# One hybrid block on one core: routing weights in four copies in DRAM, v rows straight from the plain normalised rows

## The chip, the core and the metric

The kernel runs on one core of a Trainium2 chip. A core has a matrix engine (TensorE, in the profile PE, with its weight loads as PEld), a vector engine (VectorE, DVE), a scalar engine with table functions (ScalarE, ACT), a general engine (GpSimd, POOL) and a queue that issues transfers (SyncE, SP). Each works through its own instructions in order; between engines they wait on semaphores. The metric is the device time of one execution in microseconds, lower is better. Before the change the median of three runs is 1353.25 us (1351.0 to 1355.0).

## What is computed

Eight sequences (B = 8) of 512 rows of 128 numbers pass through four residual layers: a selective scan ("mamba"), a mixture of eight experts, a windowed attention with 16 heads of 8, and the mixture of experts again, with the same weights.

```python
x = x + mamba(_layernorm(x))
x = x + ffn(_layernorm(x))
x = x + attention(_layernorm(x))
x = x + ffn(_layernorm(x))

# ffn: every expert sees every row
router_probs = softmax(x @ w_router)
gate_weights = softmax(x @ w_gating / 0.1)
g = einsum('bsh,ehf->ebsf', x, w_gate)          # 8 experts, 128 -> 512
u = einsum('bsh,ehf->ebsf', x, w_up)
h = silu(g) * u
expert_out = einsum('ebsf,efh->ebsh', h, w_down)   # 512 -> 128
cw = router_probs * gate_weights
cw = cw / (sum(cw) + 1e-9)
out = einsum('ebsh,bse->bsh', expert_out, cw)

# attention: q, k, v = x W + b; windowed softmax; out @ Wo + bo
```

Everything is fp32, and every expert is computed for every row, so the expert products are most of the arithmetic.

## The kernel before

**Precision.** A product of two fp32 matrices is made from three products in a faster format: `matmul3` (lines 489 to 494) splits both sides into a high and a low part (fp32r) and adds high x high, low x high and high x low. Small products use plain fp32.

**Layers and buffers.** Activations lie transposed in SBUF (128 features x 512 rows of a sequence). Between layers a sequence's rows are written to DRAM and read again.

**The expert stream** (`ffn_stream`, 1123 to 1325) is the backbone: for both passes k, eight sequences b, eight experts e and four chunks f of 128 hidden units, it makes g and u (three 128x512 products each), then, two to four chunks later (SHALLOW and DEPTH), the chunk's part of y. In `hidden` (1246) ACT takes the silu, DVE multiplies by u, ACT or DVE casts the high part, POOL or DVE makes the low part. The first sequence runs its first four experts in two halves of 256 rows, so that it can start earlier.

**Routing weights.** `ffn_prep` (1023 to 1100) normalises the rows, transposes them (`tp_f`), makes the logits (`lps`, `rps`), the softmaxes, and the combined weights cw, which are laid out for each tile of 128 rows with the eight experts beside each other. They are transposed (`cps`), copied to SBUF (`cwt`) and written to a DRAM tile `cwd` of 4 tiles x 8 experts x 128. For each expert, `spreads` (1197 to 1214) later reads its 512 weights back from DRAM into all 128 partitions (`cwb`), in pieces of 128 weights; the read is issued when the stream reaches the expert's last chunk and a buffer is free. `weighted` (1138) multiplies y by it on DVE and adds it to `acc` on POOL (for the first expert it writes acc directly, and y's PSUM bank is free then).

**Attention.** `attention_prep` (1341 to 1398) normalises a sequence's rows, transposes them (`tp_a`) and splits them into high and low parts. Then come q (`aqk..._0`) and k (`aqk..._1`): `matmul3`, a bias, a split into three bf16 pieces, written to DRAM in twelve transfers (`put`). Then v: `matmul3` into `avp`, bias on ACT into `avf`, four transposes into `avt`, a copy on ACT into `avs`, and one transfer `avd` to DRAM. The buffers of tag "rest" (`arest`, `avf`, `avs`) are one and the same. `attention` (1420 to 1708) reads q, k and v back for windows of about 100 queries, makes scores twice (`as` for the maxima, `aw` for the weights), and the weighted values (`ao`); `joined` (1613) makes the output product `aout`.

**Who sets the order.** The order of every engine's instructions is written out at build time by a planner in the kernel's own source: `Clock` (133 to 250) holds an estimate of when each engine is done, from costs of its own; `Lanes` (285 to 373) holds generators ("lanes"), each of which yields the engine that it needs next. `tick` runs whichever lane can start soonest. A lane that needs TensorE waits, beside its inputs, a while for other small products that it may stand next to (`joins`, by default JOIN; JOIN_MAX for the rows of maxima, JOIN_ATT for `attention_prep`), unless it is due. `HELD`, `SECOND`, `PRESS` and `FIRST` say by how much one kind of lane may go ahead of another; `SECOND` is that of the second half of the first sequence. Where TensorE would stand idle, filler products are put: `warm` ones before the stream starts, and `idle` ones after a planned gap of WARM_GAP, up to the stream position WARM_TO (1.0 is one sequence). `Clock.run` also estimates when a transfer lands. These estimates decide only the order; on the chip, semaphores do.

Two helpers that the steps name: `normalised` (542 to 563) makes the transposed rows in two parts, and with `plain=True` also a plain fp32 copy of them in the normalised rows' buffer; that buffer exists once (LNB = 1) and is passed on with `lanes.give("ln", ...)`. `load_x` and `store_x` (448, 457) move a sequence's rows.

Of the kernel before, what the change touches and what calls it, by code (L numbers as in the profile page):

```python
# [8 lines left out]
F32 = mybir.dt.float32  # L9
# [3 lines left out]
AF = mybir.ActivationFunctionType  # L13
ALU = mybir.AluOpType
# [4 lines left out]
P = 128  # L19
# [68 lines left out]

TABLES = {AF.Silu: (18,), AF.Exp: (0, 6), AF.Ln: (6,), AF.Tanh: (0, 18)}
INF = float("inf")  # L90
LAGS = {"T": 0.2, "A": 0.15, "V": 0.15, "P": 0.08}
TO_PE = 0.11
SAME = 0.125
# [2 lines left out]
FIRST = 0.6  # L96
LATE = 0.3
SIDE = 0.5
JOIN = 2.0
JOIN_DUE = 0.0  # L100
JOIN_MAX = 6.0
JOIN_ATT = 3.0
JOIN_END = 2.0
MOST = 6
OTHERS = 4
AT_FIRST = 7
WARM = 3.5
WARM_GAP = 0.25
WARM_TO = 1.5
SECOND = 0.2  # L110
PRESS = 0.4
HELD = 0.18
MAMBA_DUE = 0.9
PREP_DUE = 0.9
ATT_LEAD = 2.5
# [13 lines left out]
class Clock:  # L129
# [105 lines left out]
    def run(self, key, name, out, args, kw, after, wait):  # L235
        c = self.cost(key, name, out, args, kw)
        start = max(self.end[key] + wait, after, self.now if key == "T" else self.based(key))
        if key == "T":
            if start > self.end["T"] + 2.4:
                self.cold = start  # L240
            if start < self.cold + 3.4:
                c *= 2
        if key in "VP" and self.shares(key, name, out, args):
            start = self.with_port(start, c)
        self.end[key] = start + c
        if key == "S":
            start = max(start, self.now)
            row = out.shape[-1]
            rows = out.shape[0] * size(out) // row
            each = max(row * (2 if out.dtype == BF16 else 4), 512)  # L250
            move = rows * each / 200e3
            self.moved = max(self.moved, start + c + 0.8) + move
            return self.moved + 0.6 + move
        self.hop[key] = start + c
        return start + c + LAGS[key]

# [121 lines left out]
def block_kernel(ctx: ExitStack, tc: tile.TileContext, x, pack_a, pack_b, pack_c, w_qkv, mask, mask_t, w_o,  # L378
# [52 lines left out]
    def side(shape, name):  # L431
        return (yield from sides((shape, name)))[0]
# [590 lines left out]
    def ffn_prep(k, b, xc, t0=0, nt=NT):  # L1023

        nm = f"f{k}_{b}_{t0}"
        cols = slice(t0 * P, (t0 + nt) * P)

        def halves():
            if t0 == 0:
                ready[k, b] = [fp.tile([P, L], F32R, tag=f"xt{i}", name=f"xt{i}_{nm}") for i in range(2)], 0  # L1030
            return [t[:, cols] for t in ready[k, b][0]]

        if (k, b, t0) == (0, 0, 0):
            done["quiet"] = 0.0
        *_, xf = yield from normalised(xc, nm, halves, nt, t0 + nt == NT, quick=nt < NT, plain=True)
        if (k, b, t0) == (0, 0, 0):
            done.pop("quiet", None)
            done["calm"] = 0.0
        if t0 == 0:
            done["cw", k, b] = dram.tile([NT, NE, P], F32, tag="cwd", name=f"cwd_{nm}", bufs=3), 0.0, 0  # L1040
        cwd = done["cw", k, b][0]
        ready[k, b] = ready[k, b][0], cols.stop
        wr, = routes

        lps = yield from side([P, P], f"lps_{nm}")
        for t in range(nt):
            e = pe.matmul(lps[32 * t : 32 * t + 32], wr, xf[:, t * P : (t + 1) * P], start=True, stop=True)
        lanes.give("ln", e)
        yield "V"
        n = 32 * nt  # L1050
        lt = fp.tile([P, P], F32, tag="lt", name=f"lt_{nm}", bufs=1)
        freed(dve.tensor_copy(lt[:n], lps[:n]))
        yield "T"
        rps = yield from side([P, NT, 32], f"rps_{nm}")
        pe.transpose(rps.rearrange("p t c -> p (t c)")[:, :n], lt[:n], ident[:n, :n])
        yield "V"
        pr = fp.tile([P, 2 * NT, NE], F32, tag="pr", name=f"pr_{nm}")
        s8 = fp.tile([P, 2 * NT], F32, tag="s8", name=f"s8_{nm}")
        pr, s8 = pr[:, : 2 * nt], s8[:, : 2 * nt]
        prv = pr.rearrange("p (t s) e -> p t s e", s=2)  # L1060
        s8v = s8.rearrange("p (t s) -> p t s", s=2)
        logits = rps[:, :nt, : 2 * NE].rearrange("p t (s e) -> p t s e", s=2)
        dve.tensor_reduce(s8v, logits, AX.X, ALU.max)
        yield "V"
        freed(dve.tensor_tensor(prv, logits, s8v[:, :, :, None].to_broadcast([P, nt, 2, NE]), ALU.subtract))

        yield lambda: clock.table in TABLES[AF.Exp] or pos[0] >= k * B + b - LATE
        yield "A"
        act.activation(pr, pr, AF.Exp)
        if (k, b) == (0, 0) and t0:  # L1070
            clock.hold = clock.now


        yield "V"
        cw = fp.tile([P, NT, NE], F32, tag="cw", name=f"cw_{nm}")[:, :nt]
        s4 = fp.tile([P, NT], F32, tag="s4", name=f"s4_{nm}")[:, :nt]
        z = fp.tile([P, NT], F32, tag="z", name=f"z_{nm}")[:, :nt]
        dve.tensor_reduce(s8, pr, AX.X, ALU.add)
        pool.tensor_tensor(cw, prv[:, :, 0], prv[:, :, 1], ALU.mult)
        yield "V"  # L1080
        dve.tensor_reduce(s4, cw, AX.X, ALU.add)
        pool.tensor_tensor(z, s8v[:, :, 0], s8v[:, :, 1], ALU.mult)
        pool.tensor_scalar(z, z, 1e-9, 1.0, ALU.mult, ALU.mult)
        yield "P"
        pool.tensor_tensor(s4, z, s4, ALU.add)
        yield "V"
        dve.reciprocal(s4, s4)
        yield "P"
        pool.tensor_tensor(cw, cw, s4[:, :, None].to_broadcast([P, nt, NE]), ALU.mult)
        yield "T"  # L1090
        cps = yield from side([NT * NE, P], f"cps_{nm}")
        n = nt * NE
        pe.transpose(cps[:n], cw.rearrange("p t e -> p (t e)"), ident)
        yield "V"
        cwt = fp.tile([NT * NE, P], F32, tag="cwt", name=f"cwt_{nm}")
        freed(dve.tensor_copy(cwt[:n], cps[:n]))
        yield "S"
        e = sp.dma_start(out=cwd[t0 : t0 + nt].rearrange("t e p -> (t e) p"), in_=cwt[:n])
        done["cw", k, b] = cwd, e, cols.stop

    pos = [0.0]
# [21 lines left out]
    def ffn_stream():  # L1123
# [73 lines left out]
        def spreads():  # L1197

            for k in range(2):
                for b in range(B):  # L1200
                    todo = passes(k, b)
                    for i, (e, cs) in enumerate(todo):
# [6 lines left out]
                        n = cs.stop - cs.start  # L1209
                        cwb = fp.tile([P, L], F32, tag="cwb", name=f"cwb{k}_{b}_{e}_{cs.start}", bufs=2)[:, :n]  # L1210
                        state["cwb", (k, b, e, cs.start)] = cwb, sp.dma_start(
                            out=cwb.rearrange("p (t q) -> p t q", q=P),
                            in_=cwd[None, cs.start // P : cs.stop // P, e, :].to_broadcast([P, n // P, P]),
                        )

        def chunks(cs):
# [111 lines left out]
    def attention_consts():  # L1328
        raw = qp.tile([P, 3, P], F32, tag="rest", name="wqkv")
        there = sp.dma_start(out=raw, in_=w_qkv) + 1.5  # L1330
        yield "A", there
        consts = []
        for i, nm in enumerate(("wq", "wk", "wv")):
            consts.append((yield from split_const(raw[:, i, :], P, nm)))
            yield "A"
        return consts

    scaling = HD ** -0.5
# [2 lines left out]
    def attention_prep(b, consts):  # L1341
# [2 lines left out]
        def halves():  # L1344
            return [qp.tile([P, L], F32R, tag=f"t{i}", name=f"axt{b}_{i}") for i in range(2)]

        xt = yield from normalised(xc, f"a{b}", halves)
        stacks = []
        for m, (bcol, order) in enumerate(((B_BQ, Q_PIECES), (B_BK, K_PIECES))):
            pp = yield from side([P, L], f"aqk{b}_{m}")  # L1350
# [7 lines left out]
            def put(piece, pi):  # L1358
                js = [j for j, o in enumerate(order) if o == pi]
                places = slice(js[0], js[-1] + 1, js[1] - js[0] if len(js) > 1 else 1)  # L1360
                for s in range(2):
                    half = piece[64 * s : 64 * s + 64, None, :]
                    sp.dma_start(
                        out=qd[s, places].rearrange("j r t -> r j t"),
                        in_=half.to_broadcast([64, len(js), L]),
                    )

            ps_ = [qp.tile([P, L], BF16, tag="pc", name=f"apc{b}_{m}_{i}", bufs=3) for i in range(3)]
            rest = qp.tile([P, L], F32, tag="rest", name=f"arest{b}_{m}")
# [7 lines left out]
            dve.tensor_tensor(ps_[2], rest, ps_[1], ALU.subtract)  # L1377
            put(ps_[1], 1)
            yield "S"
            put(ps_[2], 2)  # L1380
            stacks.append(qd.rearrange("s j (d p) t -> s (j d) p t", p=NPAIR))
            yield "T"
        vp = yield from side([P, L], f"avp{b}")
        matmul3(vp, consts[2], xt)
        yield "A"
        vf = qp.tile([P, L], F32, tag="rest", name=f"avf{b}")
        freed(act.activation(vf, vp, AF.Identity, bias=pb[:, B_BV : B_BV + 1]))
        yield "T"
        vt = yield from side([P, NT, P], f"avt{b}")
        for t in range(NT):  # L1390
            pe.transpose(vt[:, t, :], vf[:, t * P : (t + 1) * P], ident)
        yield "A"
        vs = qp.tile([P, NT, P], F32, tag="rest", name=f"avs{b}")
        freed(act.copy(vs, vt))
        yield "S"
        vd = dram.tile([L, P], F32, tag="vd", name=f"avd{b}", bufs=2)
        e = sp.dma_start(out=vd.rearrange("(t p) d -> p t d", p=P), in_=vs)
        heads[b] = stacks[0], stacks[1], vd, e + 3.0

    def attention_preps():  # L1400
# [460 lines left out]
```

## Time and profile before

| | |
|---|---|
| runs | 1351.0, 1353.25, 1355.0 us (median 1353.25) |
| profiled execution | 1351.62 us, its span 1349.8 us, mean granted clock 0.996 |
| first expert product (g) | starts at 34.31 us of the span |
| expert products u, g, y | 451.5, 448.3, 445.5 us busy |
| h on POOL | 640.0 us busy in 492 additions of 1310 ns |
| table loads on ACT | 109 and 16 under another line |
| transfers | 107.75 MB, 80 GB/s over the span; the 124 reads of cwb 256 KB each |
| packets under 2 KB | 226616 of 230861 |

How to read it: the profile is one execution, taken by the hardware profiler. "Busy" is the time in which an engine worked on an instruction; matmuls are pipelined, so the durations of successive ones overlap, and their start-to-start distance says what one costs. Nearly all instructions carry line 269, since a helper there issues them; groups are told apart by the names of their tiles, output first ("avt<-ident,avf": into avt, from the identity and avf). A number in brackets behind "idle before" is how long the engine stood idle ahead of a group, with who released it. The granted clock is the share of TensorE's clock that the chip let through.

### The profile page before, as it was taken

The numbers are of one execution on the slowest core, as the hardware profiler recorded it, in microseconds if no ns is written. First come the engines' busy times: TensorE is split into PE (matmuls) and PEld (weight loads), VectorE is DVE, ScalarE is ACT, GpSimd is POOL, SyncE is SP. The second block draws the span as 40 slices with busy tenths as digits, with TensorE's granted clock in tenths as the row PEclk, the third lists the DMA queues.
The fourth block names the chain that finished last, engine by engine and source line by source line (L and its number), as shares of the span: only waits on it lengthen the run. The fifth ranks groups of instructions, "written<-read, shape, count | busy, mean of one in ns | idle before, by whom it ended". The sixth has DMA issues, their size and how long they took to land.

```text
span 1349.8 us, 29533 instructions
## 1 busy us (share of the span) xinstructions
PE 1328.9 (98%) x10261; PEld 1053.3 (78%) x10261; DVE 1036.8 (77%) x3114; ACT 964.7 (71%) x1694; POOL 940.4 (70%) x1042
## 2 busy tenths in 40 slices
PE   7999999999999999999999999999999999999998
PEld 7877778788788877777777777777777777778887
DVE  6887888688888867898788887888888787855443
ACT  7768576867787556777777777777877767765654
POOL 5877576776767757666766767767677676777776
PEclk9999999999999999999999999999999999999999
DMA  3321304232112242344345444454544434222111
GB/s 126 95 72 38 87 24 101 62 81 73 45 48 56 63 85 54 73 97 118 79 103 111 99 106 100 104 109 89 118 91 104 119 71 88 61 69 55 40 40 40
DMA packets 230861, 107.75 MB, mean 80 GB/s; under 512 B 86417, under 2 KB 226616, under 8 KB 230712
## 3 DMA queue, kind: packets, MB, share of 16 engines
q1 hardware_dynamic: 230712, 105.87, 33.9%
q8 instruction: 81, 1.33, 0.4%
q14 instruction: 68, 0.56, 0.1%
HBM read 77.64 MB, written 27.79 MB: 78 GB/s over the span
## 4 chain that ended last, share of the span: by engine, by line
PE 89%; POOL 3%; ACT 3%; issue 3%; DVE 2%; DMA 0%; POOLq 0%; DVEq 0%
PE u L269 25%; PE y L269 25%; PE g L269 25%; PE ao L269 2%; PE aw L269 2%; PE as L269 2%; POOL h L269 1%; PE mo L269 1%; PE aqk L269 1%; ACT h L269 1%; DVE h L269 1%; PE mde L269 1%; PE aout L269 1%; PE yp L269 1%; ACT L269 1%
## 5 line engine op out<-in xcount | busy, mean ns | idle before, releaser
L269 POOL TENSOR_TENSOR h<-h,h 128x512 fp32r<-128x512 f32 x492 | 640.0, 1310 | 279.0 <-ACT h L269 219.4
L269 PE MATMUL u<-xt_f,wu 128*128 128x512 f32 (+1 forms) x1584 | 451.5, 395 | 3.5 <-ACT h L269 2.7
L269 PE MATMUL g<-xt_f,wg 128*128 128x512 f32 (+1 forms) x1584 | 448.3, 393 | 2.1 <-ACT h L269 1.9
L269 PE MATMUL y<-h,wd 128*128 128x512 f32 (+1 forms) x1584 | 445.5, 392 | 1.4 <-POOL h L269 0.8
L269 DVE TENSOR_TENSOR h<-u,h 128x512 f32<-128x512 f32 x420 | 285.9, 686 | 157.5 <-PE u L269 109.3
L269 ACT ACTIVATE h<-g 128x512 f32<-128x512 f32 x512 | 303.4, 597 | 123.2 <-PE g L269 100.1
L269 ACT CAST h<-h 128x512 fp32r<-128x512 f32 x437 | 268.4, 619 | 171.2 <-DVE h L269 169.6
L269 PEld LDWEIGHTS g<-xt_f,wg 128*128 128x128 f32 x1584 | 288.5, 189 | 70.3 <-ACT h L269 3.0
L269 PEld LDWEIGHTS y<-h,wd 128*128 128x128 f32 x1584 | 288.3, 188 | 70.2 <-POOL h L269 1.4
L269 PEld LDWEIGHTS u<-xt_f,wu 128*128 128x128 f32 x1584 | 286.6, 189 | 71.7 <-ACT h L269 4.1
L269 POOL TENSOR_TENSOR acc<-acc,cwb 128x512 f32<-128x512 f32 (+1 forms) x114 | 148.0, 1298 | 52.5 <-DVE cwb L269 33.8
L269 ACT ACT_TABLE_LOAD x109 | 139.8, 1283 | 24.7 <-PE g L269 23.2
L269 DVE CUSTOM_DVE_ANT_0 amasked<-as,maskq 128x60 f32<-128x60 f32 x640 | 95.4, 213 | 5.0 <-PE as L269 4.8
L269 DVE TENSOR_TENSOR cwb<-y,cwb 128x512 f32<-128x512 f32 (+1 forms) x116 | 77.5, 668 | 16.0 <-PE y L269 14.4
L269 DVE TENSOR_TENSOR apt<-aw,maskk 125x400 f32<-125x400 f32 (+2 forms) x160 | 88.1, 570 | 0.0
L269 DVE SCALAR_TENSOR_TENSOR h<-h,g 128x512 f32<-128x512 f32 x92 | 62.3, 681 | 27.0 <-ACT h L269 26.6
L269 ACT ACTIVATE apt<-apt 125x400 f32<-125x400 f32 (+2 forms) x160 | 81.5, 540 | 0.4
L269 DVE SCALAR_TENSOR_TENSOR h<-u,h 128x512 f32<-128x512 f32 x92 | 62.6, 683 | 3.3 <-PE g L269 0.5
L269 DVE DVE_READ_ACCUMULATOR2_ANT amx<- 128x1 f32 x640 | 52.1, 81 | 0.0
L269 DVE CAST h<-h 128x512 fp32r<-128x512 f32 x75 | 48.8, 651 | 1.2
L269 DVE COPY v<-avr 125x128 f32<-125x128 f32 (+2 forms) x40 | 25.7, 644 | 26.4 <-PE ao L269 26.4
L269 PEld LDWEIGHTS ao<-apt,v 125*32 125x32 f32 (+2 forms) x1280 | 27.4, 109 | 14.6 <-DVE h L269 4.4
(205 smaller groups left out, 1239.5 us busy)
## 6 DMA issues: line engine op xcount, KB each, us to landing
cwb<-cwd_f SPq DMA_DIRECT2D x124, 256.0 KB
aqd<-apc SPq DMA_DIRECT2D x32, 192.0 KB
ks<-aqd SPq DMA_DIRECT2D x48, 93.8 KB
x_fo<-x SPq DMA_DIRECT2D x16, 256.0 KB
aqd<-apc SPq DMA_DIRECT2D x32, 128.0 KB
x_f<-x SPq DMA_DIRECT2D x15, 256.0 KB
qs<-aqd SPq DMA_DIRECT2D x48, 75.0 KB
aod<-aos SPq DMA_DIRECT2D x24, 100.0 KB
```

The lines of the kernel that those rows point to most:

```text
L269: f(*args, **kw)
```

## The change

1. Routing weights: cw is laid out in SBUF with each expert's tiles beside each other, `cwd` becomes copies x 8 experts x 4 tiles x 128, and, for a whole sequence, one transfer writes four copies of it (for the first sequence's halves there is one copy). An expert's weights are then one piece of 512 numbers, and the read into 128 partitions takes each group of 32 partitions from another copy.
2. v: the weight matrix of v stays one plain fp32 matrix, its bias is spread once over all partitions (`abv`, `bv`). For each tile of 128 rows, one plain fp32 product with the normalised rows as the stationary side gives v's rows directly, without transposes; DVE adds the bias and `avd` is written. This stands ahead of q and k, and the normalised rows' buffer is passed on after v's products.
3. The planner's numbers: joins are waited for longer, fillers come after a longer gap and up to a later position, two of the lanes' advantages are smaller, and a transfer is estimated to land 0.8 us after its data moved, with the move counted once.

```diff
+COPIES = 4
...
-JOIN = 2.0
+JOIN = 3.0
 JOIN_DUE = 0.0
-JOIN_MAX = 6.0
-JOIN_ATT = 3.0
+JOIN_MAX = 10.0
+JOIN_ATT = 8.0
...
-WARM_GAP = 0.25
-WARM_TO = 1.5
-SECOND = 0.2
+WARM_GAP = 0.5
+WARM_TO = 2.5
+SECOND = 0.1
 PRESS = 0.4
-HELD = 0.18
+HELD = 0.15
...
-            self.moved = max(self.moved, start + c + 0.8) + move
-            return self.moved + 0.6 + move
+            self.moved = max(self.moved, start + c + 0.6) + move
+            return self.moved + 0.8
...
-            done["cw", k, b] = dram.tile([NT, NE, P], F32, tag="cwd", name=f"cwd_{nm}", bufs=3), 0.0, 0
+            copies = COPIES if nt == NT else 1
+            done["cw", k, b] = dram.tile([copies, NE, NT, P], F32, tag=f"cwd{copies}", name=f"cwd_{nm}", bufs=3), 0.0, 0
...
-        cw = fp.tile([P, NT, NE], F32, tag="cw", name=f"cw_{nm}")[:, :nt]
+        cw_rows = fp.tile([P, NE * NT], F32, tag="cw", name=f"cw_{nm}")[:, : NE * nt]
+        cw = cw_rows.rearrange("p (e t) -> p t e", e=NE)
...
-        pe.transpose(cps[:n], cw.rearrange("p t e -> p (t e)"), ident)
+        pe.transpose(cps[:n], cw_rows, ident)
...
-        e = sp.dma_start(out=cwd[t0 : t0 + nt].rearrange("t e p -> (t e) p"), in_=cwt[:n])
+        if nt == NT:
+            e = sp.dma_start(
+                out=cwd.rearrange("r e t p -> (e t) r p"), in_=cwt[:, None, :].to_broadcast([n, COPIES, P])
+            )
+        else:
+            e = sp.dma_start(out=cwd[0, :, t0 : t0 + nt, :], in_=cwt[:n])
...
-                            out=cwb.rearrange("p (t q) -> p t q", q=P),
-                            in_=cwd[None, cs.start // P : cs.stop // P, e, :].to_broadcast([P, n // P, P]),
+                            out=cwb,
+                            in_=cwd[:, None, e, cs.start // P : cs.stop // P, :]
+                            .rearrange("r o t q -> r o (t q)")
+                            .to_broadcast([cwd.shape[0], P // cwd.shape[0], n]),
...
-        for i, nm in enumerate(("wq", "wk", "wv")):
+        for i, nm in enumerate(("wq", "wk")):
             consts.append((yield from split_const(raw[:, i, :], P, nm)))
             yield "A"
+        wv = const.tile([P, P], F32, name="wv")
+        act.copy(wv, raw[:, 2, :])
+
+        wide = qp.tile([P, P], F32, tag="t0", name="bvs")
+        yield "P"
+        pool.tensor_copy(wide, pb[:, B_BV : B_BV + 1].to_broadcast([P, P]))
+        yield "T"
+        bp = yield from side([P, P], "abv")
+        pe.matmul(bp, wide, ident, start=True, stop=True)
+        bv = const.tile([P, P], F32, name="bv")
+        yield "A"
+        freed(act.copy(bv, bp))
+        consts += wv, bv
...
-        xt = yield from normalised(xc, f"a{b}", halves)
+        *xt, xf = yield from normalised(xc, f"a{b}", halves, plain=True)
+        vt = yield from side([P, NT, P], f"avt{b}")
+        for t in range(NT):
+            e = pe.matmul(vt[:, t, :], xf[:, t * P : (t + 1) * P], consts[2], start=True, stop=True)
+        lanes.give("ln", e)
+        yield "V"
+        vs = qp.tile([P, NT, P], F32, tag="rest", name=f"avs{b}")
+        freed(dve.tensor_tensor(vs, vt, consts[3][:, None, :].to_broadcast([P, NT, P]), ALU.add))
+        yield "S"
+        vd = dram.tile([L, P], F32, tag="vd", name=f"avd{b}", bufs=2)
+        v_end = sp.dma_start(out=vd.rearrange("(t p) d -> p t d", p=P), in_=vs)
+        yield "T"
...
-        vp = yield from side([P, L], f"avp{b}")
-        matmul3(vp, consts[2], xt)
-        yield "A"
-        vf = qp.tile([P, L], F32, tag="rest", name=f"avf{b}")
-        freed(act.activation(vf, vp, AF.Identity, bias=pb[:, B_BV : B_BV + 1]))
-        yield "T"
-        vt = yield from side([P, NT, P], f"avt{b}")
-        for t in range(NT):
-            pe.transpose(vt[:, t, :], vf[:, t * P : (t + 1) * P], ident)
-        yield "A"
-        vs = qp.tile([P, NT, P], F32, tag="rest", name=f"avs{b}")
-        freed(act.copy(vs, vt))
-        yield "S"
-        vd = dram.tile([L, P], F32, tag="vd", name=f"avd{b}", bufs=2)
-        e = sp.dma_start(out=vd.rearrange("(t p) d -> p t d", p=P), in_=vs)
```

More of the change, by code (lines that the diff above doesn't have):

```diff
@@ L1362, in put @@
                     half = piece[64 * s : 64 * s + 64, None, :]
-                    sp.dma_start(
+                    end = sp.dma_start(
                         out=qd[s, places].rearrange("j r t -> r j t"),
@@ L1366, in put @@
                     )
+                return end
             ps_ = [qp.tile([P, L], BF16, tag="pc", name=f"apc{b}_{m}_{i}", bufs=3) for i in range(3)]
@@ L1379, in attention_prep @@
             yield "S"
-            put(ps_[2], 2)
+            e = put(ps_[2], 2)
             stacks.append(qd.rearrange("s j (d p) t -> s (j d) p t", p=NPAIR))
             yield "T"
-        vp = yield from side([P, L], f"avp{b}")
-        matmul3(vp, consts[2], xt)
-        yield "A"
-        vf = qp.tile([P, L], F32, tag="rest", name=f"avf{b}")
-        freed(act.activation(vf, vp, AF.Identity, bias=pb[:, B_BV : B_BV + 1]))
-        yield "T"
-        vt = yield from side([P, NT, P], f"avt{b}")
-        for t in range(NT):
-            pe.transpose(vt[:, t, :], vf[:, t * P : (t + 1) * P], ident)
-        yield "A"
-        vs = qp.tile([P, NT, P], F32, tag="rest", name=f"avs{b}")
-        freed(act.copy(vs, vt))
-        yield "S"
-        vd = dram.tile([L, P], F32, tag="vd", name=f"avd{b}", bufs=2)
-        e = sp.dma_start(out=vd.rearrange("(t p) d -> p t d", p=P), in_=vs)
         heads[b] = stacks[0], stacks[1], vd, e + 3.0
```

## The prediction

> **What bounds the kernel now.** I read the page first: busy shares, then the 40 slices and the chain.
>
> ```profile
> span 1349.8 us, 29533 instructions
> PE 1328.9 (98%) x10261; PEld 1053.3 (78%) x10261; DVE 1036.8 (77%) x3114; ACT 964.7 (71%) x1694; POOL 940.4 (70%) x1042
> ...
> PE   7999999999999999999999999999999999999998
> ...
> PE 89%; POOL 3%; ACT 3%; issue 3%; DVE 2%; DMA 0%; POOLq 0%; DVEq 0%
> ```
>
> TensorE is full nearly everywhere, and the chain is TensorE for 89% of the span. So the end is the start of the expert stream, plus the sum of TensorE's instructions, plus its stalls; what the other engines do counts only where TensorE waits for it. Who it waits for:
>
> ```profile
> PE u L269 <- ACT h L269: 2.7, 3, 1.4
> PE mbx L269 <- DVE mst L269: 2.6, 1, 2.6
> ...
> PE g L269 <- ACT h L269: 1.9, 1, 1.9
> ```
>
> No DMA is among TensorE's waits. Stretches around two stalls (columns: stretch, busy time of PE, PEld, DVE, ACT, POOL, granted clock, DMA share, GB/s) show what a stall costs besides itself:
>
> ```profile
> 67.00:70.80 3.80, 2.65 (x10) 1.27 (x9) 3.35 (x10) 3.72 (x6) 1.37 (x2) 1.00 0.01 3
> 70.80:74.20 3.40, 3.40 (x14) 3.01 (x14) 2.54 (x8) 3.39 (x8) 2.60 (x5) 0.51 0.27 77
> ...
> 172.00:176.60 4.60, 2.66 (x14) 1.86 (x12) 2.44 (x5) 4.54 (x8) 3.55 (x3) 1.00 0.10 26
> 176.60:180.00 3.40, 3.40 (x8) 2.73 (x9) 2.47 (x4) 2.16 (x4) 1.76 (x2) 0.51 0.18 42
> ```
>
> After TensorE stood idle a good part of 4 us, the granted clock is half for 3.4 us: 1.7 us lost, twice. Record by record I compared each matmul's start-to-start distance with the median for the same two kinds: from 34 to 270 us TensorE is 21 us behind those medians, from 270 to 506 us only 4.5. So what can be won beyond plain work lies in the first three sequences.
>
> **The change, part by part.**
>
> *v rows.* The rows at stake:
>
> ```profile
> L269 PE MATMUL avp<-axt,wv_hi 128*128 128x512 f32 x16 | 6.5, 406 | 0.0
> L269 PE MATMUL avt<-ident,avf 128*128 128x128 f32 x32 | 5.1, 281 | 0.3 <-DVE h L269 0.2
> ...
> 231.86 0.39 PE L269 MATMUL mo<-pa,macc 128*128 128x128 f32 x2
> 232.08 0.60 PE L269 MATMUL avt<-ident,avf 128*128 128x128 f32 x4
> ```
>
> Durations of pipelined matmuls overlap, so I use distances: the 512-wide products follow each other at 231 ns, transposes at 109 ns; a plain fp32 128x128 product (mo) is two records 111.5 ns apart, 223 ns. Removed per sequence: 3 x 231 + 4 x 109 = 1129 ns; added: 4 x 223 = 892. Saved 0.237 x 8 = 1.9 us; the once-made bias block adds 0.2. On ACT per sequence, avf 0.69 and avs 0.59 go and a 0.49 copy comes; DVE gets one 0.69 addition. In all, with 19 h casts moved to ACT (0.52 each) and four more table loads (1.28 each), ACT gains some 8 us of 965, POOL 7 additions of 1.30; both are about 70% busy, priced at nothing. Without that cover it would be those 8 or 9 us.
>
> v now comes ahead of q and k: avd's DMA (issue 0.37) stands before the twelve aqd issues on SP, and q and k come some 10 us of products later. For the first sequence the attention's first value load is at 492 us and its preparation near 200, so nothing waits; if that cover were gone, attention and not the stream would be late. The buffer "rest" is now refilled by q's remainder after avd has landed (2.3 to 6.0 us in the trace's landing events); seven sequences have 7 to 12 us of products between, the fourth 3.5. There DVE can wait up to 3 us, with h products queued behind it; TensorE has two to four finished chunks in hand, so 0, bound 3.
>
> *Order on TensorE.* In the built programs, maximal runs of small products between 512-wide ones fall from 201 to 185, and joins of a small product directly behind an attention or routing run rise from 30 to 40. A return to 512-wide products costs their first one 320 instead of 232 ns; a small run alone costs no more than its transposes. So 10 x 0.089 = 0.9 us saved.
>
> *Start.*
>
> ```profile
> 26.36 1.30 POOL L269 TENSOR_TENSOR wg<-stageg,wg 128x512 fp32r<-128x512 f32 x1 [8.62 <-ACT wg L269]
> ...
> 28.93 1.30 POOL L269 TENSOR_TENSOR wd<-staged,wd 128x512 fp32r<-128x512 f32 x1
> 30.31 0.19 POOL L269 TENSOR_SCALAR va_f<-mv_f 128x2 f32<-128x2 f32 x1
> ...
> 33.89 0.36 PE L269 MATMUL idle<-sel 128*128 128x256 f32 x1
> 34.31 0.98 PE L269 MATMUL g<-xt_f,wg 128*128 128x256 f32 x6
> ```
>
> The statistics were there at 29.57 us, but POOL had three weight remainders ahead. ACT now casts wg2 ahead of a pair of exponentials, so POOL does its remainder in its 8.6 us of idleness and is free by 29.5: 0.7 us. The filler before the first g is gone: 0.4. Sum 1.1; from 0 (the second half-sequence sets the pace anyway) to 1.5.
>
> *Early stalls.* Filler products after the start fall from 30 to 18, but the gap from which one is put rises from 0.25 to 0.5 us: 30 x 0.25 = 7.5 us at least before, 18 x 0.5 = 9 after. This is no sign of fewer stalls. Against that, 1.4 to 3.5 us more expert work now stands ahead of each product of the second sequence's scan (35.2 against 33.1 us ahead of its output product); what DVE's chain times is then less waited for. I take 2.0 saved, nearer the second row. Bounds: 9 saved (somewhat under half of the 21) to 6 lost (two new stalls of 1.3 with the 1.7 us of half clock each).
>
> By the Trainium skill (TensorE: Matmul & The Clock Gate, HAM oscillation) only idle gaps beyond some 3.4 us lower the clock; by it the two half-clock stretches above would not be and would price at 0. The wait of 1.9 us ahead of g that ended at 176.6 did lower it, so the row decides: 3.4 us at stake.
>
> *Routing weights.* cwd is written four times over, 64 KB instead of 16: landing from 2.05 us (its own median) to 3.0 (avd's 256 KB). The broadcast read stays 256 KB: its packets are 2 KB (107 ns mean) instead of 512 B (35): 128 x 107 / 16 = 0.86 against 512 x 35 / 16 = 1.12 us of engine time. It landed after 5.35 us (median). Bounds afterwards: 4.2 (weights' 2 KB rows) to 5.8 (the 127-row v load, whose semaphore rose in 2 events where the others' rose in 16, 63 KB on what looks like one engine). What this hides behind:
>
> ```profile
>   DMA cwb<-cwd_f: 0.5, 2
> ```
>
> Half a microsecond of waiting in all: worth 0 while the read comes early enough. The skill (DMA: Bandwidth & Descriptors, "Why a DMA increments its semaphore by 16 and not by 1") speaks against the edit: the leading dimension of both sides sets how many engines share a transfer, and the source now leads with 4. By it the read lands at the upper bound, without it at the lower; the sum is the same by either.
>
> *Sum.* -1.9 + 0.2 - 0.9 - 1.1 - 2.0 = -5.7 us. The profiled execution took 1351.6 (span 1349.8 and 1.8 around it), so 1345.9 there; the median, 1353.25, is 1.6 above it: **1347.5**.
>
> **Rivals.**
>
> *Rows only.* The two halves of the first sequence are tied: what the start wins waits at the second half's normalisation, and the old stalls come back elsewhere. Left: 1.9 - 0.2 + 0.9 = 2.6, 1350.7. For it: filler counts show no fewer gaps. Against: the denser order.
>
> *Late routing weights* (the slow side). A preparation now holds the normalised rows' single buffer until v is made, and joins wait longer, so in the second pass the FFN preparations of sequences 2 to 5 (counted from 1) slip: from the transposition of their rows to their first g stand 5.5 us of products (before 9 to 12), from the routing transposition to the end of their first y 11.3 (before 16 to 17). Before, the first broadcast landed 8 to 16 us after that transposition, and was wanted at 18 to 21. If it still lands at 14, DVE waits about 3 us in four sequences, with the h products queued behind; passed on whole, 12 us: 1353.25 - 3.7 + 12 = 1361.5. Against: the read is issued at a position of the stream, so the later of these landings did not wait for data (the one near 953 us came after 7.9). It decides from 11.3 us on, and from DVE waits for cwb of over 5 us in all.
>
> *All early stalls halved.* 9 instead of 2: 1340.5.
>
> **How the numbers follow.** Forecast 0.50 (1343 to 1349), halved stalls 0.05, rows only 0.25, late weights 0.20. Range 1341 to 1359: it leaves out the end of the late weights and part of the 0.05. From the same cases, with 0.3% (4 us, about what this measurement tells from none): faster 0.55, within 0.25, slower 0.20.
>
> **What will show it.** v: avt records 64 at 111 ns, no avp. Start: va_f near 29.6, first g near 33.2. Stalls: half-clock stretches after 34 us fewer than two, and TensorE's sum of waits under ACT h below 5. Late weights: DVE cwb or acc waiting for cwb's DMA, and TensorE short of work around 780, 866, 953 and 1040 us. I am wrong if TensorE's busy time falls by 3 us and the span does not, or if stalls appear past 270 us.

## The result, and the profile after

The changed kernel takes 1399.31 us (median of 5, 1394.36 to 1400.48), the kernel before beside it 1352.81: a ratio of 1.033 (1.031 to 1.036), slower by 46.5 us. Forecast was 1347.5, with 1359 as the upper end: wrong in sign. The profiled execution is the slowest of the five and has the lowest mean granted clock (0.982; the others 0.985 to 0.987), so its stretches at half clock are somewhat longer than theirs. The page of the changed kernel:

```profile
span 1398.7 us, 29500 instructions
PE 1347.7 (96%) x10249; PEld 1064.0 (76%) x10249; DVE 1030.1 (74%) x3103; ACT 971.0 (69%) x1705; POOL 946.6 (68%) x1050
...
PE 78%; DMA 6%; ACT 5%; DVE 4%; POOL 3%; issue 2%; SPq 1%; POOLq 0%; DVEq 0%; ACTq 0%
```

The span grew by 48.9 us in two parts. TensorE stands idle for 51.0 us (1398.7 - 1347.7) where it was 20.9. And it is busy 18.8 us longer with 12 instructions fewer. Its clock was halved for 51.2 us of the span instead of 10.2 (the profile's clock records, summed); half of the difference, some 20 us by this estimate, accounts for it. Transfers, at 0% of the old chain, now hold 6% of the new one. Who waits for them (columns: us in all, times, longest):

```profile
DVE acc L270 <- DMA cwb<-cwd_f: 20.7, 4, 5.8
PE u L270 <- DVE acc L270: 13.8, 4, 4.0
DVE cwb L270 <- DMA cwb<-cwd_f: 7.7, 3, 3.3
...
PE as L270 <- DMA ks<-aqd: 3.8, 4, 1.2
```

The first two lines are one event, four times: DVE needs the first expert's routing weights to write `acc`, the products with u queue behind it on DVE, and TensorE runs out of free banks. One of the four, first on SP's queue, then on DVE, then on TensorE (timelines: start, duration, engine, line and operation; in brackets the idle time before it and who ended it):

```profile
817.17 0.54 SPq L270 DMA_DIRECT2D cwd_f<-cwt_f  x1
...
822.34 0.52 SPq L270 DMA_DIRECT2D cwb<-cwd_f  x1
```

```profile
830.99 0.69 DVE L270 TENSOR_TENSOR acc<-y,cwb 128x512 f32<-128x512 f32 x1 [5.66 <-DMA cwb<-cwd_f]
```

```profile
826.91 0.86 PE L270 MATMUL g<-xt_f,wg 128*128 128x512 f32 x3
831.73 1.32 PE L270 MATMUL u<-xt_f,wu 128*128 128x512 f32 x3 [3.96 <-DVE acc L270]
```

The write of the weights is issued at 817.17 us and lands 1.9 us later. The read is issued 5.2 us after the write, since seven other issues stand between them on SP, and lands 8.55 us after that; DVE stands for 5.66 us, TensorE for 3.96. What follows (columns as before: stretch, PE, PEld, DVE, ACT, POOL, clock, DMA share, GB/s):

```profile
822.34:831.00 8.66, 5.43 (x91) 3.89 (x89) 2.75 (x20) 5.89 (x10) 2.77 (x3) 1.00 0.50 138
832.00:835.50 3.50, 3.50 (x34) 2.52 (x37) 3.07 (x16) 0.62 (x1) 1.12 (x5) 0.52 0.40 126
```

The wait is followed by a stretch at half clock, another 1.7 us. Where the time went, by the first g of each sequence (us; first and second pass through the stream; the last row ends with TensorE's last product):

| stretch | before | after | difference |
|---|---|---|---|
| up to the first g | 34.3 | 36.0 | +1.7 |
| first pass, sequences 1 to 6 | 491.1 | 494.2 | +3.1 |
| first pass 7 and 8, second pass 1 (attention under way) | 254.3 | 276.0 | +21.7 |
| second pass 2 to 5 (the four waits) | 342.9 | 365.3 | +22.4 |
| second pass 6 to 8 | 223.9 | 223.7 | -0.3 |

The attention's first products run at 488 us before and 518 us after, its last at 1217 and 1265. In the first and the last rows little changes. The loss lies in the two rows between, where the attention's transfers and the reads of the routing weights are issued side by side.

In the row of the four waits both kernels run 3576 matmuls. After the change TensorE is idle 14.7 us more there, 13.8 of it the four waits, and busy 7.7 us more, with 17.1 us at half clock: that is the whole of the 22.4. In the row above it is idle 10.6 us more, 13.7 us pass at half clock, and 91 more matmuls fall into the stretch.

### The profile page after: what moved, and what is told of

Its sections match the earlier page's. It is cut to its first block, busy times and chain, and to the rows that moved or that the text cites. A ratio compares the mean times of both kernels' runs of the same rounds, so it can differ in the third digit from the quotient of the medians.

```text
span 1398.7 us, 29500 instructions
## 1 busy us (share of the span) xinstructions
PE 1347.7 (96%) x10249; PEld 1064.0 (76%) x10249; DVE 1030.1 (74%) x3103; ACT 971.0 (69%) x1705; POOL 946.6 (68%) x1050
## 4 chain that ended last, share of the span: by engine, by line
PE 78%; DMA 6%; ACT 5%; DVE 4%; POOL 3%; issue 2%; SPq 1%; POOLq 0%; DVEq 0%; ACTq 0%
PE u L270 22%; PE y L270 22%; PE g L270 21%; DMA cwb<-cwd_f 3%; PE ao L270 2%; ACT h L270 2%; PE aw L270 2%; POOL h L270 2%; PE as L270 1%; PE mo L270 1%; SPq L270 1%; ACT L270 1%; DVE h L270 1%; DMA ks<-aqd 1%; DMA x_a<-x 1%
## 5 line engine op out<-in xcount | busy, mean ns | idle before, releaser
L270 POOL TENSOR_TENSOR h<-h,h 128x512 fp32r<-128x512 f32 x499 | 647.8, 1309 | 287.1 <-ACT h L270 239.3
L270 PE MATMUL u<-xt_f,wu 128*128 128x512 f32 (+1 forms) x1584 | 453.1, 396 | 20.3 <-DVE acc L270 13.8
L270 ACT CAST h<-h 128x512 fp32r<-128x512 f32 x456 | 279.3, 619 | 218.1 <-DVE h L270 216.1
L270 DVE TENSOR_TENSOR h<-u,h 128x512 f32<-128x512 f32 x417 | 282.3, 686 | 166.3 <-PE u L270 107.4
L270 PEld LDWEIGHTS y<-h,wd 128*128 128x128 f32 x1584 | 292.5, 191 | 74.0 <-issue 3.2
L270 POOL TENSOR_TENSOR acc<-acc,cwb 128x512 f32<-128x512 f32 (+1 forms) x114 | 144.9, 1271 | 58.6 <-DVE cwb L270 54.6
L270 DVE SCALAR_TENSOR_TENSOR h<-h,g 128x512 f32<-128x512 f32 x95 | 64.1, 681 | 21.3 <-ACT h L270 21.3
L270 DVE COPY v<-avr 125x128 f32<-125x128 f32 (+2 forms) x40 | 22.3, 557 | 23.1 <-PE ao L270 23.0
L270 PE MATMUL ao<-apt,v 125*32 125x100 f32 (+2 forms) x1280 | 39.2, 267 | 0.0
```

The costliest lines, as they stand in the source:

```text
L270: f(*args, **kw)
```

## The experiments

Three edits sit in the change: the layout of the weights (W), v's rows (V), the planner's numbers (P). In the traces W alone leaves every engine's order as it is, with one exception. With V under the old planner, the write of four copies is estimated to land later, and in second-pass sequences 3 and 5 the first read of weights stands behind one more issue on SP (1.1 us) and their first use 16 instructions later on DVE; TensorE's order stays. So runs that differ in W alone compare transfers, and in that one case (v_only against after_old_planner, and one copy against four) nearly so.

### First round: layout, width of its read, planner

*w_only*: the kernel before with W. *after_old_weights*: the changed kernel without W (both by the hunks on `cwd`, `cw_rows` and `cwb` shown above). *after_wide_read*: the changed kernel with one edit, so that neighbouring partitions read different copies and the dimension of 32 leads:

```diff
-in_=cwd[:, None, e, ...].rearrange("r o t q -> r o (t q)").to_broadcast([cwd.shape[0], P // cwd.shape[0], n])
+in_=cwd[None, :, e, ...].rearrange("o r t q -> o r (t q)").to_broadcast([P // cwd.shape[0], cwd.shape[0], n])
```

*after_old_planner*: the changed kernel without P:

```diff
-JOIN = 3.0
+JOIN = 2.0
-JOIN_MAX = 10.0
-JOIN_ATT = 8.0
+JOIN_MAX = 6.0
+JOIN_ATT = 3.0
-WARM_GAP = 0.5
-WARM_TO = 2.5
-SECOND = 0.1
+WARM_GAP = 0.25
+WARM_TO = 1.5
+SECOND = 0.2
-HELD = 0.15
+HELD = 0.18
...
-            self.moved = max(self.moved, start + c + 0.6) + move
-            return self.moved + 0.8
+            self.moved = max(self.moved, start + c + 0.8) + move
+            return self.moved + 0.6 + move
```

> The kernel before with the new layout of the routing weights alone (four copies, an expert's in one piece); every engine's order stays that of before, row for row, only the shapes of 149 transfers change. Theory A (the order lost the time: the planner's numbers and v's new place put the routing weights and the attention's reads too near to where they are wanted): the reads land some 0.2 to 2 us later on fewer queues, but they had 8 to 16 us in hand, so 1350 to 1358 us, DVE waits for cwb's DMA under 3 us. Theory B (the narrow read lost it: 5 landing events where there were 16, and it holds up what shares its queues): 1375 us or more, with DVE waiting for cwb over 10 us.

> The changed kernel with the routing weights laid out and read as before; every engine's order is that of the changed kernel, row for row. Theory A: the reads land a little earlier (median 5.35 instead of 5.55 us, at most 7.0 instead of 9.5), each of the four long waits for cwb in the second pass shrinks by at most 3 us, and some of the half-clock stretches behind them go: 1375 to 1397 us. Theory B: 1350 to 1360 us.

> The changed kernel with the same four copies, but neighbouring partitions read from different copies, so that the read's leading dimension is 32 instead of 4; order row for row that of the changed kernel. Both theories expect the landing events of cwb to go from 5 to 16. Theory A: the landing shortens to 4.5 us or so, 1375 to 1397 us. Theory B: 1350 to 1362 us. If the landing events stay at 5, the leading dimension is not what sets the width.

> The changed kernel, layout and v rows as changed, with the planner's seven numbers and its estimate of a landing as before. Theory A: waits for cwb's DMA under 5 us in all, no half-clock stretches past 270 us, 1347 to 1356 us. Theory B: the narrow read stays, so 1375 us or more.

Measured: 1354.04, ratio 1.0008 (0.9999 to 1.0018); 1378.0, 1.018 (1.017 to 1.020); 1364.99, 1.008 (1.007 to 1.010); 1374.04, 1.014 (1.012 to 1.017). Neither theory stands, though 1378.0 is within A's range. W costs nothing on the order of before (against B), yet on the changed order the wide read wins 34 us (against A), and with the old planner 20 us stay (against A again). That the read of the change is narrow shows in the profile. The page's line on packets, of the changed kernel and of the same order with the wide read:

```profile
DMA packets 182204, 108.47 MB, mean 78 GB/s; under 512 B 84961, under 2 KB 162088, under 8 KB 182056
```

```profile
DMA packets 183644, 108.48 MB, mean 79 GB/s; under 512 B 86401, under 2 KB 163528, under 8 KB 183496
```

The data are the same; the wide read has 1440 small packets more (of 4 bytes each), 12 for each of the 120 reads of whole sequences that start from four copies. The semaphore of such a read rises in 5 steps when narrow and 16 when wide. The Trainium skill (DMA: Bandwidth & Descriptors, "Why a DMA increments its semaphore by 16 and not by 1") says that each participating engine ends with its own write to the semaphore and that the leading dimension of both sides sets how many take part: 4 against 16 make 12 writes a read, which agrees. Landing of the first weights of second-pass sequences 2 to 5 (issue to last landing event, us):

```
before             5.34  5.48  4.79  5.48
changed, old W     5.21  5.58  7.50  5.94
changed (narrow)   8.55  7.78  8.59  7.18
changed, wide      4.45  4.21  4.47  4.82
```

Over all reads the medians hide this: 5.35 before, 5.55 narrow (but up to 9.53), 3.89 wide.

### Second round: each part alone

*w16_only*: the kernel before with W and the wide read; *v_only* and *planner_only*: with V or P alone; *after_old_planner_wide*: V and W with the wide read, old planner.

> The kernel before with the four copies and the wide read (leading dimension 32); every engine's order as before, row for row. Theory N (the narrow read does harm only where an order has little in hand, and the order of before has 8 to 16 us): 1350 to 1355 us, with cwb landing after 3.9 us instead of 5.35; the faster read brings nothing. Rival (transfers set some of the time of before as well): 1348 us or less.

> The kernel before with v's rows made as changed; layout of the weights and the planner as before. Every engine's order is that of the run with the old planner (1374.0 us), row for row. Theory N: the 20 us of that run come from the narrow read meeting an order with less in hand, so here 1352 to 1360 us. Rival V (v's products ahead of q and k, with the normalised rows' one buffer held for them, cost it by themselves): 1365 to 1374 us.

> The kernel before with the planner's seven numbers and its estimate of a landing as changed; layout and v as before. The changed kernel with the old layout took 1378.0 us: v and planner together cost 25. Theory N: most of that is the planner's, which waits longer for joins and believes that a transfer of 256 KB lands 1.3 us earlier: 1365 to 1376 us, with waits of DVE and TensorE for DMAs. Rival V: 1352 to 1358 us.

> The run with the old planner (1374.0 us), with the wide read; its order row for row. Theory N: 1350 to 1358 us, cwb's landing 3.9 us, DVE's waits for cwb's DMA from 21 us to under 5, waits for aover under 3. Rival V: 1362 us or more. If it lands under 1350, it beats the kernel before.

Measured: 1352.77, ratio 0.9996 (0.9987 to 1.0006); 1357.83, 1.003 (1.001 to 1.005); 1364.26, 1.008 (1.007 to 1.010); 1352.0, 0.999 (0.998 to 1.000). Theory N holds on the order of before, where the wide read brings nothing, and for V: V costs 5 us with the old read, 21 with the narrow, nothing with the wide one. (The 22 us between narrow and wide, 1374.0 and 1352.0, are in one and the same order.) P alone costs 11, just under N's range. Transfers that DVE waits for, old planner with V, first narrow, then wide:

```profile
DVE cwb L270 <- DMA cwb<-cwd_f: 15.0, 10, 3.3
DVE aover L270 <- DMA aover<-aod: 9.1, 5, 2.5
DVE acc L270 <- DMA cwb<-cwd_f: 6.0, 2, 3.4
DVE arest L270 <- DMA avd<-avs: 2.9, 1, 2.9
```

```profile
DVE cwb L270 <- DMA cwb<-cwd_f: 1.0, 2, 0.5
DVE aover L270 <- DMA aover<-aod: 0.8, 2, 0.4
DVE acc L270 <- DMA cwb<-cwd_f: 0.7, 2, 0.5
```

The narrow read also delays others: `aover` (16 KB, 9 landing events) lands within 8.12 us in nine cases of ten, with the wide read within 3.80, in the same order.

### Third round: the held buffer, and the planner's two halves

V keeps the normalised rows' only buffer until its products are done, and the routing preparation of the next sequence waits for that buffer. *old_planner_own_buffer* puts the plain copy elsewhere:

```diff
-        *xt, xf = yield from normalised(xc, f"a{b}", halves, plain=True)
+        def own():
+            return qp.tile([P, L], F32, tag="rest", name=f"axf{b}")
+
+        *xt, xf = yield from normalised(xc, f"a{b}", halves, plain=own)
...
-        lanes.give("ln", e)
```

(`normalised` then gives "ln" away after the transposes and copies into that tile.) With this edit the planner writes another order for every engine, so such a run shows the buffer together with the new order. *wide_own_buffer* has the wide read as well. *wide_old_landing* and *wide_old_numbers* are after_wide_read with one half of P undone: the estimate of a landing, or the seven numbers.

> The run with the old planner and the narrow read (1374.0 us), with the plain copy of the attention's rows in the buffer of tag rest instead of in the normalised rows' own, so that this is passed on after the transposes, as before the change. In the built order the distance from the routing transposition to the end of the first y in the second pass goes from 8.6, 9.9, 8.6, 9.9 us of products (sequences 2 to 5) to 19.8, 17.0, 15.6, 12.8. Theory H (the held buffer makes the routing late, and only then the narrow read costs): 1351 to 1360 us, DVE's waits for cwb's DMA from 21 us to under 6. Rival Q (what costs is how the narrow read shares its few queues with the attention's transfers, wherever the routing stands): 1366 us or more.

> The same with the wide read: the version in which every cost found so far is taken out. Theory H: 1347 to 1353 us, about the 1352.0 of the run with the held buffer, since the wide read already covers the short distance. Rival Q: the same; it says nothing between the two.

> The changed kernel with the wide read (1365.0 us) and the planner's old estimate of a landing, its seven numbers as changed. Theory L (the new estimate is 1.3 us too short for 256 KB, so the order puts TensorE's products and DVE's work where their data have not landed): 1351 to 1357 us. Rival J (the longer joins and later fillers cost): 1361 to 1368 us.

> The counterpart: the changed kernel with the wide read, the planner's seven numbers as before and its new estimate of a landing. Theory L: 1361 to 1368 us, TensorE waiting for ks near 515, 580 and 668 us as with both. Rival J: 1351 to 1357 us.

Measured: 1356.97, ratio 1.002 (1.001 to 1.004); 1353.7, 1.0004 (0.9994 to 1.0014); 1360.7, 1.006 (1.004 to 1.007); 1369.29, 1.012 (1.010 to 1.014). Theory H's numbers came (the second run lies 0.7 above its range): with the buffer given back, the narrow read costs 3 us instead of 22. The new order by itself is no faster, as the wide read shows (1353.7 against 1352.0). What DVE waits for there:

```profile
DVE cwb L270 <- DMA cwb<-cwd_f: 4.8, 3, 2.2
```

Of P, neither L nor J is right alone. From 1352.0 (neither half) the estimate alone adds 17, the numbers alone 9, both 13; each half costs and they do not add. The waits with the new estimate alone show reads that come too late, those of rows for the preparations (`x_a`, `x_f`) above all:

```profile
DVE st_a L270 <- DMA x_a<-x: 9.6, 5, 2.4
DVE cwb L270 <- DMA cwb<-cwd_f: 5.5, 3, 3.9
DVE st_f L270 <- DMA x_f<-x: 3.8, 3, 2.3
```

With the old estimate in its place and nothing else changed (1352.0) these three are 1.1 us, 1.0 and nothing. Which of the seven numbers costs was not tried.

### Fourth round: the same under the changed planner, and one copy

*after_own_buffer* and *after_wide_own*: the changed kernel with the own buffer, narrow and wide. *one_copy_wide*: after_old_planner_wide with

```diff
-COPIES = 4
+COPIES = 1
```

> The changed kernel, narrow read and changed planner, with the plain copy of the attention's rows in the buffer of tag rest, so that the normalised rows' buffer is passed on after the transposes. In the built order the second pass's distance from the routing transposition to the end of the first y goes from 11.3 us of products in sequences 2 to 5 to 21.6, 25.9, 21.4, 21.6. Theory H (held buffer times narrow read is most of the loss under this planner too): 1358 to 1370 us, DVE's waits for cwb's DMA from 28 us to under 8, no half-clock stretch past 800 us. Rival (the planner's numbers and estimate carry most of it, through the attention's reads): 1380 us or more.

> The same with the wide read. What stays is the planner's own cost: it was 11.4 us on the kernel before (1364.3) and 13 with v changed and the wide read (1365.0 against 1352.0). Theory H: 1358 to 1366 us. Rival: 1350 to 1357 us (the planner's numbers cost only because of the held buffer).

> The run with the old planner and the wide read (1352.0 us, cwb landing after 3.9 us) with one copy in DRAM instead of four: the read's leading dimension is 128, all partitions from the same 2 KB; TensorE's order as there. Theory (the width alone matters): landing events 16, landing 3.7 to 4.2 us, 1350 to 1354 us. Rival (128 partitions reading one place are slowed, which is what the copies are for): landing above 5 us, 1358 us or more.

Measured: 1378.79, ratio 1.020 (1.018 to 1.021); 1362.95, 1.008 (1.006 to 1.010); 1351.27, 0.998 (0.997 to 0.999). For the first, H's range was too low, and the rival's end is only 1 us off; one half-clock stretch also came past 800 us (near 1120), where H expected none. The second lies in H's range, the third in its theory's. The waits for cwb did fall, from 28.4 us to 7.0, but others took their place, those for `aover` first (6.6 us in the changed kernel):

```profile
DVE aover L270 <- DMA aover<-aod: 15.5, 6, 4.7
DVE st_f L270 <- DMA x_f<-x: 7.7, 4, 2.5
DVE st_a L270 <- DMA x_a<-x: 7.4, 6, 2.0
DVE cwb L270 <- DMA cwb<-cwd_f: 7.0, 4, 5.7
```

With the wide read in the same order `aover` is waited for 5.3 us. So giving the buffer back is worth 20 us, and widening the read another 16. One copy, read by all 128 partitions from the same 2 KB, lands after 3.71 us (median) with 16 events: the copies aren't needed once the read is wide. This is the lowest median of the study, 2.5 us below the 1353.79 of the kernel before beside it; its 0.7 us below four copies (1352.0) are not told from none:

```profile
span 1347.2 us, 29504 instructions
PE 1326.9 (98%) x10268; PEld 1051.7 (78%) x10268; DVE 1042.7 (77%) x3112; ACT 961.1 (71%) x1695; POOL 942.7 (70%) x1046
...
PE 93%; issue 2%; POOL 2%; DVE 2%; ACT 1%; POOLq 0%; ACTq 0%
```

### Fifth round: does P alone make the narrow read cost?

*planner_narrow* and *planner_wide*: planner_only with W, narrow and wide.

> The kernel before with the planner's numbers and estimate as changed (1364.3 us) and the narrow read, v as before; order of every engine that of that run. Theory M (the narrow read costs wherever the order leaves the reads little time, and the changed estimate alone makes such an order): 1374 to 1384 us. Rival (v's new place is needed for it): 1362 to 1368 us.

> The same order with the wide read. Both: 1360 to 1365 us, since the wide read lands 1.5 us earlier than that of before; by theory M a few us below the 1364.3 of the old layout.

Measured: 1365.33, ratio 1.009 (1.008 to 1.011); 1360.11, 1.006 (1.004 to 1.007). Theory M falls: without V the narrow read costs P's order 1 us against the old layout, as it does on the order of before, and 5 us against the wide read. All medians together (us; the kernel before, beside these runs, took 1352.8 to 1353.8):

| | old planner, old v | old planner, V | P, old v | P and V |
|---|---|---|---|---|
| old layout | 1353 | 1357.8 | 1364.3 | 1378.0 |
| W, narrow read | 1354.0 | 1374.0 | 1365.3 | 1399.3 |
| W, wide read | 1352.8 | 1352.0 | 1360.1 | 1365.0 |
| narrow, V's buffer given back | | 1357.0 | | 1378.8 |
| wide, V's buffer given back | | 1353.7 | | 1363.0 |

With the old layout P alone costs 11.4 us, V alone 5.0 and both together 25.2, so 8.8 come from their meeting; the narrow read adds 21.3 on top, 46.5 in all. What stays open: why V under P, with its buffer given back, still pays 16 us for the narrow read (the line of `aover` suggests that narrow transfers hold each other up, no run separates it), and which chain loses the 21.7 us between 530 and 806 us. There the changed planner with the wide read loses 12.9 us; with the own buffer besides it is 4.1, with the old planner instead 0.3; so buffer and planner act together, but no wait of the page carries more than 8 us of it.

## Why the prediction was wrong, point by point

**The routing weights (0).** This step failed: "worth 0 while the read comes early enough", and of the two bounds for its landing "the sum is the same by either". In place of 0 the narrow read cost 21.3 us on the changed order against the old layout (1399.3 and 1378.0) and 34.3 against the wide read. The median landing, 5.55 us, did lie within 4.2 to 5.8, and the write of four copies landed after 1.8 us (median) and not 3.0. But the price was taken at a median and on the order of before. In the four places where the time was short, the narrow read took 7.2 to 8.6 us, while seven other transfers were issued. The row was there: the v load with its two landing events (the other v loads rose in 6 or 12, not in 16), and the rule on the leading dimension that the prediction itself names. They were weighed, but the narrow read was never set against the shortened distance as one cost.

**Late routing weights (chance 0.20).** The mechanism is the one that happened: same four sequences, same wait on DVE; with the held buffer given back, the waits for cwb fall from 28.4 us to 7.0. It was foreseen near 780, 866, 953 and 1040 us, where these sequences began before; TensorE fell idle at 828, 920, 1011 and 1104, 21 to 22 us into sequences that began 26 to 45 us later. Its size was not foreseen: 12 us were set, 22.4 measured in this stretch. Missing were the longer landing (5.35 assumed), and the half clock that followed the waits (17.1 us of it, 8.5 lost).

**The planner's order (-0.9 for joins, -2.0 for early stalls).** These terms failed too, in sign: P alone costs 11.4 us. Products standing nearer together were read from the order, but not what they then wait for. In the first pass's sequences 1 to 6, planner_only loses 6.3 us and the changed kernel 3.1, where a gain was set. Announced were fewer than two half-clock stretches after 34 us and under 5 us of TensorE's waits for ACT's h; measured were eleven and 9.1 us. Eight of the eleven lie past 270 us, which the prediction had named as a sign of being wrong. That the new landing estimate is shorter than what transfers take (256 KB in 3.3 us by the planner, 3.89 even with the wide read) could be read from the diff and the page of before, and was given no price.

**v rows (-1.7).** The products are as announced:

```profile
L270 PE MATMUL avt<-wv,xn_a 128*128 128x128 f32 x64 | 8.8, 282 | 0.0
```

64 records, 112 ns apart, no avp. Their gain shows only where nothing else is lost: with the wide read and the old planner 1352.0 against 1352.8 without V. That is 0.8 us, less than the runs can resolve; it neither confirms nor refutes the 1.7.

**The "rest" buffer (0, bound 3).** Held: the changed kernel shows no such wait; the longest of any run was 2.9 us, with V and the old planner (the `arest` line above).

**The start (-1.1).** Not seen: the first g stood at 36.01 us, not near 33.2. POOL's order came as foreseen, but the step took `va_f`'s inputs as given:

```profile
32.44 0.19 POOL L270 TENSOR_SCALAR va_f<-mv_f 128x2 f32<-128x2 f32 x1 [1.75 <-DVE mv_f L270]
```

POOL is idle and waits for DVE's statistics, so `va_f` ran at 32.44 and not 29.6. In the same order with the wide read it ran at 30.27, and on before's order at 30.31, 31.06 and 32.52 in three runs. A term of 1.1 us can't be told from one profile of this start.

**"All early stalls halved" and "Rows only"** did not come about; the second (1350.7) is near what W and V give with a wide read and the old planner (1352.0).

## What to carry to other kernels

Read a transfer's leading dimension before its bytes: the same 256 KB landed in 5 steps with a source that led with 4 and in 16 with one that led with 32, and this one swap gave 34 us here. Price a transfer at its worst landing in the crowd where it is wanted, together with everything in the same change that shortens the time in hand; taken alone, the narrow read cost 1 us and V 5. When a change has three parts, build the table of all combinations: the layout of the change cost 1 us on one order and 21 us on another.

## What the runs showed of the hardware

- The clock was halved behind short waits: in the 5 us before 740 us TensorE stood idle for 2.0 in all, and lost 1.7 more in the stretch behind. Not every such wait did it: one of 1.45 us that ended at 265.4 us of the kernel before was followed by full clock. The Trainium skill (TensorE: Matmul & The Clock Gate, HAM oscillation) warns of idle gaps beyond some 3.4 us; these rows show half clock after less, and they decide:

```profile
735.00:740.00 5.00, 2.99 (x14) 1.97 (x12) 1.89 (x4) 1.22 (x2) 1.29 (x1) 1.00 0.71 118
740.00:743.40 3.40, 3.38 (x8) 2.71 (x9) 2.95 (x6) 2.24 (x3) 1.28 (x1) 0.50 0.44 85
```

- 128 partitions reading one and the same 2 KB of DRAM were not slower (3.71 us, median) than reading four copies of it (3.82, same width and the same order on TensorE).
- The time from the span's start to the first g varies by 2.5 us between profiles of one order (33.85, 36.01 and 36.31 us for the changed one).
